# A Fourier-operator kernel on one Trainium2 core: the sum over h as two matmuls on 64-column tiles of the array instead of one on all 128 columns

## The chip, the core and the metric

One core of one Trainium2 chip runs the whole program. The metric is device microseconds of one execution. A core has a tensor engine (PE; its weight loads are listed apart, as PEld), a vector engine (DVE), a scalar engine (ACT), POOL, and SP, which here only starts DMAs. [...]

## What is computed

The input is x of shape (2, 56, 128, 128): 2 x 56 = 112 images of 128 x 128. Two layers, each x = x + conv(gn(x)), all in float32. Cut to what matters:

```python
def spectral_conv(x, w, b):            # 32 x 16 Fourier modes are kept
    xf = rfft2(x, norm='forward')
    of[:, :, :16, :16]  = einsum('bihw,iohw->bohw', xf[:, :, :16, :16],  w[0])
    of[:, :, -16:, :16] = einsum('bihw,iohw->bohw', xf[:, :, -16:, :16], w[1])
    return irfft2(of) + b
def fno_layer(x, ...):                 # spectral_conv + 1x1 skip, with norm and gelu as asked
def conv(x):
    xn = inorm(x)                      # per image
    k, q, v = fno_layer(xn) three times, 8 heads
    out = softmax(q k / 128) v         # attention over the 56 images of a batch entry
    out = fno_layer(out)
    att = inorm(out + x); an = inorm(att)
    h = gelu(inorm(spec(an)) + skip(an))      # M0
    h = inorm(spec(h)) + skip(h)              # M1
    return inorm(h) + att
```

## The kernel before

All planes stay in SBUF as `[h, image, w]`: X is the residual, A the work plane, 112 images each. Everything linear is carried in the 32 x 16 modes, so a plane is transformed forwards three times in a layer (for attention, M0 and M1) and back three times. A transform is two sums, each a matmul with a constant matrix of cosines and sines.

`to_rows` (line 265) is the first sum, over h. For eight images at a time it takes a PSUM tile `py` of 128 x 512 from the pool `pm` of four banks; for each image one matmul has the plane `A[:, i + e, :]` (128 x 128: h on partitions, w in columns) as the stationary operand and the constant `fh` (128 x 64: real and imaginary part of 32 rows of ky) as the moving one, and writes 64 columns of the tile with w on the 128 partitions (line 270). Then `evict` copies the tile to `Y`, on DVE (line 126) and ACT (line 128) in turn. `to_modes` (line 274) is the second sum, over w: eight matmuls of 32 output columns per half, on four column tiles of the array (line 282), then a swap of real and imaginary part (line 289). `from_modes` goes back: the modes are turned by way of DRAM (lines 300, 303), POOL copies a slice of 16 images (line 308), PE sums over ky with 64 x 64 stationary pieces on two column tiles (line 312), ACT evicts (line 316), PE sums over kx (line 319), and DVE uses the result.

In a layer, line 270 runs in four places. For each half of the images (a batch entry) come group norm (lines 340 to 364), row statistics (326), the instance norm that leaves A normalized (DVE line 378, two of three images, ACT line 376, the third), and `to_rows` of that half. I call the two halves A and B. In A, PE also has the group-norm sums of the second half (line 340) to do, which do not wait for `to_rows`; in B, the inner products of the first half (line 394: 128 weights of 56 columns, each streaming 56 columns, read with a stride of 512 bytes). After them come the scores (406), softmax, transposes (421, 446), the product with the attention (453), the mix of the images (462, 467), `from_modes`, statistics (253, 261), and the scales q1 and al (485 to 494). Then the places C (`to_rows` of all 112 images for M0) and D (the same for M1). Between them DVE adds att's part to the residual (line 538, once for each image) before it may write A again (line 542); both need q1.

A scheduler sets the order of each engine's instructions when the program is built, by its own estimate of times; semaphores then only make them wait.

Of the kernel before, what the change touches and what calls it, by code (L numbers as in the profile page):

```python
"""Two pre-activation CoDA-FNO layers on x (2, 56, 128, 128), float32 throughout, on one core.

A spectral convolution is a diagonal operator on 32 x 16 Fourier modes, so everything linear is
carried in those modes and in the image axis, and the 128 x 128 plane is touched only where the
layer is not low rank:

  xh      the instance-normed plane (mean 0); q, k, v = (Spec + s) (g1 xh + b1) + bias
  scores  <q_k, k_l> by Parseval = sum over modes of conj(xh_k) U xh_l  +  sq sk <xh_k, xh_l>
          with U = conj(wq + sq) (wk + sk) - sq sk
  out     the attention mixes images and Spec acts on modes, so they commute:  # L10
          P(attn v) = ISpec(sum_a T_a attn_a xh) + (sum_a sp sv attn_a) xh + constants
          with T = (wp + sp) (wv + sv) - sp sv
  M0, M1  the norm of Spec(x) is taken on its coefficients (its mean is the DC coefficient plus
          the bias M0b / M1b, which the norm subtracts again)

irfft2 takes the real part at kx = 0, which makes the multiplier there Hermitian:
w~(ky) = (w(ky) + conj w(-ky)) / 2, and w / 2 at ky = -16, whose mirror +16 carries the other half.
All of these are identities.

Layouts.  planes: [h, image, w].  modes: partition p = 32 j + 16 c + kx, free (t, image), where  # L20
c = re / im and 8 j + t is the row of ky in (0..15, -16..-1).
"""

# [15 lines left out]
I = B * K  # L39
HEADS = 8  # L40
EPS = 1e-5
HALF = 4 * I  # the images of four t: one PSUM bank

# [1 line left out]
_KY = np.r_[0:16, -16:0]  # L45
# [33 lines left out]

# columns of the vector of small parameters of a layer  # L80
_COLS = {}
# [9 lines left out]
N_W = 4 * HEADS + 2  # L91


def _bc(ap, axis, n):
    """A new axis of n repeats."""
    ap = ap.unsqueeze(axis)
    shape = list(ap.shape)
    shape[axis] = n
    return ap.to_broadcast(shape)
# [3 lines left out]
def fno_layers(ctx: ExitStack, tc: tile.TileContext, x, out, weights, small, const):  # L103
# [18 lines left out]
    def evict(to, of):  # L122
        """PSUM to SBUF, on the two engines in turn."""
        turn[0] ^= 1
        if turn[0]:
            nc.vector.tensor_copy(to, of)  # L126
        else:
            nc.scalar.copy(to, of)  # L128

# [1 line left out]
    X = planes.tile([N, I, N], F32, name="X")  # L131
# [29 lines left out]

# [1 line left out]
    def prepare(layer):  # L163
# [19 lines left out]

        # images' constants: c = b1 (w(0) + s) + bias
        c24 = col(24)
# [13 lines left out]
        g.tensor_tensor(pr["p_c"], pr["p_c"], par["psb"], ALU.add)  # L199
        # products of the skips' weights  # L200
        ss, vp = col(8), col(8)
# [9 lines left out]
        g.tensor_scalar(g2n, g2, float(N), None, ALU.mult)  # L211
        # w + s
        g.tensor_tensor(W[:, 0, 0:32, :], W[:, 0, 0:32, :], _bc(sm[:, 0:32], 2, 8), ALU.add)
# [32 lines left out]

# [1 line left out]
    def image_stats(rows, mu, var):  # L248
# [14 lines left out]

# [1 line left out]
    def to_rows(Y, i0, n):  # L265
        """The sum over h, of n images from i0: [w, (c, ky), image]."""
        for i in range(i0, i0 + n, 8):
            py = pm.tile([N, 512], F32, name="mm")
            for e in range(8):
                nc.tensor.matmul(py[:, 64 * e : 64 * e + 64], lhsT=A[:, i + e, :], rhs=fh, start=True, stop=True)  # L270
            evict(Y[:, :, i : i + 8].rearrange("p m i -> p i m"), py.rearrange("p (i m) -> p i m", m=64))

    def to_modes(Y):
        """The sum over w, and a copy with re and im exchanged."""
        xf = sp.tile([N, 8, I], F32, name="spec")
        xs = sp.tile([N, 8, I], F32, name="spec")
        pf = px.tile([N, 2, 512], F32, name="two")
        for h in range(2):
            for j in range(4):
                for c in range(2):  # L280
                    m = 32 * c + 8 * j + 4 * h
                    nc.tensor.matmul(
                        pf[32 * j : 32 * j + 32, h, :HALF], lhsT=fw[:, c, :], rhs=Y[:, m : m + 4, :],
                        start=(c == 0), stop=(c == 1),
                    )
            evict(xf[:, 4 * h : 4 * h + 4, :].rearrange("p t i -> p (t i)"), pf[:, h, :HALF])
        for h in range(2):
            ps = pm.tile([N, 512], F32, name="mm")
            nc.tensor.matmul(ps[:, :HALF], lhsT=swap, rhs=xf[:, 4 * h : 4 * h + 4, :], start=True, stop=True)
            evict(xs[:, 4 * h : 4 * h + 4, :].rearrange("p t i -> p (t i)"), ps[:, :HALF])  # L290
        return xf, xs

# [1 line left out]
    def from_modes(S, use):  # L294
        # ky from the free side to partitions and kx back, by way of memory
        turned = dram.tile([64, 16, I], F32, name="turned")
# [33 lines left out]

# [1 line left out]
    def layer(par, pr, last):  # L332
        mu, var, sd, rs, sh = (vec(n) for n in ("mu", "var", "sd", "rs", "sh"))
        Y = big.tile([N, 64, I], F32, name="big")
        for b in range(B):
            lo, hi = b * K, b * K + K
            # group norm over (image, h, 4 of w)
            acc = pa.tile([N, 512], F32, name="acc")
# [23 lines left out]
            for n, i in enumerate(range(lo, hi, 4)):  # L362
                e = nc.gpsimd if n % 3 == 2 else nc.vector
                e.tensor_tensor(A[:, i : i + 4, :], A[:, i : i + 4, :], gvf, ALU.mult)  # L364
                for k in range(4):
                    rows_stats(rows, i + k, i + k - lo)
            # instance norm: A = xh, with xa = sd xh + mu
            m_, v_, s_, r_, h_ = (t[:, lo:hi] for t in (mu, var, sd, rs, sh))
# [12 lines left out]

        # U xh for each head, while the tensor engine does <xh, xh>
        UX = big.tile([N, HEADS, 8, I], F32, name="big")
# [14 lines left out]

        # attention, rows k on partitions; then its transpose, rows l on partitions
        aT, pw = [], px.tile([N, 2, 512], F32, name="two")  # L400
        for b in range(B):
# [22 lines left out]
            aT.append(sT)  # L424
            # sum_a sp sv attn_a, transposed, as a block of the mix of all images
            wm = at.tile([K, HEADS, K], F32, name="scores")
# [9 lines left out]

        # D = sum_a T_a attn_a xh
        D = sp.tile([N, 8, I], F32, name="spec")
# [18 lines left out]

        # A = mix of the images, in place, four w at a time
        for w in range(0, N, 4):
# [9 lines left out]

        # A = out + xa  # L470
        rows2 = [st.tile([N, K, 6], F32, name="rows") for _ in range(B)]
# [7 lines left out]

        # att = q1 (A - mu) + ban;  an = alpha (A - mu) + b2  # L480
        mu, var, q1, al = (vec(n) for n in ("mu", "var", "q1", "al"))
# [12 lines left out]
        nc.vector.tensor_scalar(s0, al, par["m0sw"], None, ALU.mult)  # L494
        # t0 = m0sw b2 + m0sb - s0 mu;  ca = ban - q1 mu
        nc.vector.tensor_tensor(t0, s0, mu, ALU.mult)
# [7 lines left out]
        def normed(xf, xs, n, scale, dc):  # L504
            """The coefficients of inorm(Spec(scale x)), with dc in the place of the mean."""
            y = sp.tile([N, 8, I], F32, name="spec")
# [23 lines left out]

        # M0: A = gelu(inorm(Spec(an)) + m0sw an + m0sb)
        Y = big.tile([N, 64, I], F32, name="big")
# [3 lines left out]
        for i in range(I):  # L536
            # the residual takes att's part of A before A goes
            nc.vector.scalar_tensor_tensor(X[:, i, :], A[:, i, :], q1[:, i : i + 1], X[:, i, :], ALU.mult, ALU.add)
# [9 lines left out]

        # M1: A = inorm(Spec(h)) + m1sw h + m1sb
        Y = big.tile([N, 64, I], F32, name="big")  # L550
# [11 lines left out]

        # x + att + inorm(h, gmo, bmo)
        mu, var, a3, c3 = (vec(n) for n in ("mu", "var", "q1", "c3"))
# [27 lines left out]
def _weights(inputs, layer):  # L592
    """[p = (j, c, kx), own / mirrored in ky at kx = 0, re / im, weight, t]."""
    cols = []
    for n in ("K", "Q", "V", "P", "M0", "M1"):
        w = np.asarray(inputs[f"L{layer}_conv_{n}w"])
        w = w.reshape(2, -1, 16, 16, 2)
        cols.append(np.concatenate([w[0], w[1]], 1))  # weight, ky, kx, re / im
    w = np.concatenate(cols, 0)
    m = w.copy()  # L600
    m[:, :, 0] = w[:, (-np.arange(32)) % 32, 0]
    both = np.stack([w, m], 0).reshape(2, N_W, 4, 8, 16, 2)  # own, weight, j, t, kx, re / im
    one = both.transpose(2, 4, 0, 5, 1, 3)  # j, kx, own, re / im, weight, t
    two = np.stack([one, one], 1)  # j, c, kx, ...
    return two.reshape(N, 2, 2, N_W, 8)
# [34 lines left out]
```

## Time and profile before

| | |
|---|---|
| median of three runs | 1427.12 us |
| lowest and highest | 1420.92 and 1431.49 us |
| the profiled execution, span from its first to its last instruction | 1412.7 us |
| its mean granted TensorE clock | 0.747 |
| instructions | 13545 |
| line 270: multiplies, loads | 1344, 1344 |

The profile does not give the profiled execution a time of its own beside the span; 14.4 us lie between the span and the median of the runs. The clock is granted in two steps in this profile, 0.5 and 1.0 of full speed; the mean hides long stretches of either. In the profile's rows an instruction is named by line, engine, operation and `out<-in`, then partitions x elements. A pair such as `128*64` behind the tiles' names is rows x columns of the array that a load or multiply uses. The time behind a matmul's start goes to its modelled end and overlaps the next one's, so a pace is read from the starts of a run of them, or from the run's length without the last one's duration. Brackets hold the idle time before a row and what ended it.

### The profile page before, as it was taken

To read this page: it belongs to the slowest core of one execution; us is meant where nothing else is said; L and a number is where in the kernel's file an instruction comes from. 1 tells how busy PE (TensorE), PEld (TensorE's weight loads), DVE (VectorE), ACT (ScalarE), POOL (GpSimd) and SP (SyncE) were. 2 spreads that over 40 slices of the span, in tenths; PEclk is the share of its full clock that TensorE was granted. 3 is DMA by queue.
4 is the path that set the end of the run, shared out by engine and by line. 5 is a ranking of instruction groups with operands and counts; after the bars stand their busy time and mean duration, and the time that the engine had idled before them with its cause. 6 is when DMAs were issued, how large, how long until landed. Compare 5 with 4: busy or idle time off the path is not lost.

```text
span 1412.7 us, 13545 instructions
## 1 busy us (share of the span) xinstructions
PE 1003.7 (71%) x4992; PEld 695.5 (49%) x4992; DVE 819.8 (58%) x2052; ACT 306.0 (22%) x536; POOL 211.9 (15%) x259
## 2 busy tenths in 40 slices
PE   5374899798778936948633849989877887287550
PEld 1151788346664823724212438944566556146320
DVE  2367452791116797528978581739411397873498
ACT  0222200002221203410352321010122112152024
POOL 6603040000001013011131110400000001301102
PEclk9777599665558977979866957986555599599685
DMA  9000000001000010010000000000100000100106
GB/s 260 0 1 1 0 1 1 1 0 26 0 1 1 1 27 0 1 27 1 1 0 1 0 0 1 1 0 0 26 0 1 0 1 0 27 1 1 26 16 193
DMA packets 38872, 22.89 MB, mean 16 GB/s; under 512 B 8606, under 2 KB 37654, under 8 KB 38806
## 3 DMA queue, kind: packets, MB, share of 16 engines
q1 hardware_dynamic: 37216, 20.19, 5.8%
q10 hardware_dynamic: 1590, 1.83, 0.5%
q8 instruction: 39, 0.64, 0.2%
q14 instruction: 27, 0.22, 0.1%
HBM read 11.93 MB, written 10.09 MB: 16 GB/s over the span
## 4 chain that ended last, share of the span: by engine, by line
PE 60%; DVE 22%; ACT 8%; issue 3%; DMA 3%; POOL 3%; SPq 1%; ACTq 0%; POOLq 0%; DVEq 0%
PE mm L270 12%; PE acc L394 9%; PE mm L467 9%; PE mm L319 9%; DVE rows L326 6%; PE mm L453 5%; PE acc L353 3%; PE mm L312 3%; ACT t L464 3%; DVE A L364 2%; DVE A L580 2%; DVE A L557 2%; PE mm L462 2%; PE acc L340 2%; ACT A L128 2%
## 5 line engine op out<-in xcount | busy, mean ns | idle before, releaser
L319 PE MATMUL mm<-c_gw,t 128*128 128x512 f32 x336 | 168.8, 646 | 31.1 <-ACT t L316 31.1
L270 PEld LDWEIGHTS mm<-c_fh,A 128*128 128x128 f32 x1344 | 168.7, 206 | 8.5 <-issue 3.9
L270 PE MATMUL mm<-c_fh,A 128*128 128x64 f32 x1344 | 172.8, 291 | 0.0
L467 PE MATMUL mm<-mixT,t 112*128 112x112 f32 x512 | 131.2, 438 | 46.5 <-ACT t L464 46.5
L467 PEld LDWEIGHTS mm<-mixT,t 112*128 112x128 f32 x512 | 114.1, 328 | 72.8 <-ACT t L464 72.8
L308 POOL COPY lc<-spec 64x128 f32<-64x128 f32 x84 | 52.7, 655 | 627.7 <-PE mm L312 339.0
L126 DVE COPY A<-mm 128x448 f32<-128x448 f32 x32 | 29.1, 908 | 188.2 <-PE mm L467 188.2
L326 DVE BATCH_NORM_STATS2 rows<-A 128x6 f32<-128x128 f32 x672 | 137.0, 275 | 0.1
L394 PE MATMUL acc<-A 128*56 128x56 f32 x1024 | 134.0, 312 | 0.0
L394 PEld LDWEIGHTS acc<-A 128*56 128x56 f32 x1024 | 128.6, 226 | 6.1 <-issue 3.2
L319 PEld LDWEIGHTS mm<-c_gw,t 128*128 128x128 f32 x336 | 65.2, 205 | 108.1 <-issue 52.9
L126 DVE COPY big<-mm 128x512 f32<-128x512 f32 (+1 forms) x50 | 48.2, 971 | 98.6 <-PE mm L270 98.2
L312 PE MATMUL mm<-c_gh,lc 64*64 64x128 f32 x672 | 51.1, 297 | 75.0 <-POOL lc L308 75.0
L128 ACT COPY big<-mm 128x512 f32<-128x512 f32 (+1 forms) x50 | 47.8, 956 | 204.5 <-PE mm L270 138.9
L312 PEld LDWEIGHTS mm<-c_gh,lc 64*64 64x64 f32 x672 | 40.0, 145 | 104.0 <-POOL lc L308 76.1
L353 PE MATMUL acc<-t,ones_gn 128*128 128x512 f32 x112 | 57.1, 665 | 47.6 <-ACT t L352 47.6
L453 PE MATMUL mm<-attnT,big 56*128 56x448 f32 x128 | 82.8, 822 | 3.7 <-DVE spec L454 3.6
L542 DVE SCALAR_TENSOR_TENSOR A<-A,s,mm 128x128 f32<-128x128 f32 x224 | 59.4, 341 | 28.3 <-PE mm L319 28.3
L316 ACT COPY t<-mm 128x512 f32<-128x512 f32 x42 | 24.6, 586 | 220.6 <-PE mm L312 220.6
L462 PE MATMUL mm<-c_ident,A 128*112 128x128 f32 x256 | 68.0, 421 | 0.0
L340 PE MATMUL acc<-X,ones_gn 128*128 128x512 f32 x112 | 60.4, 688 | 10.1 <-DMA X<-x 7.6
L464 ACT COPY t<-mm 112x512 f32<-112x512 f32 x64 | 37.5, 586 | 136.5 <-PE mm L462 136.5
(170 smaller groups left out, 1239.9 us busy)
## 6 DMA issues: line engine op xcount, KB each, us to landing
X<-x SPq DMA_DIRECT2D x14, 512.0 KB, 7.3
out<-X SPq DMA_DIRECT2D x28, 256.0 KB, 2.3
turned<-spec SPq DMA_DIRECT2D x48, 56.0 KB, 2.0
spec<-turned SPq DMA_DIRECT2D x12, 224.0 KB, 3.7
raw<-weights ACTq DMA_DIRECT2D x2, 544.0 KB, 5.0
c_gw<-const_gw ACTq DMA_DIRECT2D x1, 256.0 KB, 5.3
sm<-small ACTq DMA_DIRECT2D x2, 63.0 KB, 5.5
c_swap<-const_swap ACTq DMA_DIRECT2D x1, 64.0 KB, 5.7
```

The costliest lines, as they stand in the source:

```text
L126: nc.vector.tensor_copy(to, of)
L270: nc.tensor.matmul(py[:, 64 * e : 64 * e + 64], lhsT=A[:, i + e, :], rhs=fh, start=True, stop=True)
L312: nc.tensor.matmul(pz[64 * c : 64 * c + 64, N * e : N * e + N], lhsT=four, rhs=gh[:, c, :], start=True, stop=True,)
L319: nc.tensor.matmul(po, lhsT=z[:, N * e : N * e + N], rhs=gw, start=True, stop=True)
L326: nc.vector.bn_stats(rows[:, k, :], A[:, i, :])
L340: nc.tensor.matmul(acc, lhsT=ones_gn, rhs=X[:, i : i + 4, :], start=(i == lo), stop=(i + 4 == hi))
L353: nc.tensor.matmul(acc2, lhsT=ones_gn, rhs=sq, start=(i == lo), stop=(i + 4 == hi))
L394: nc.tensor.matmul(acc[:K, :K], lhsT=plane, rhs=plane, start=(w == 0), stop=(w == N - 1))
L453: nc.tensor.matmul(pv, lhsT=XT[:, b, n, t, :], rhs=aT[b], start=True, stop=True)
L462: nc.tensor.transpose(pt[:I, N * e : N * e + N], A[:, :, w + e], ident)
L464: nc.scalar.copy(xt[:I, :], pt[:I, :])
L467: nc.tensor.matmul(po[:, I * e : I * e + I], lhsT=xt[:I, N * e : N * e + N], rhs=mix, start=True, stop=True)
```

## The change

In `to_rows` each image's matmul becomes two. The plane's 128 columns of w are halved; columns 0 to 63 go to the first 64-column tile of the array and to PSUM partitions 0 to 63, columns 64 to 127 to the second tile and to partitions 64 to 127. Both stream the same 64 columns of `fh`. What is computed, the PSUM tiles and the evictions are the same. All comments are gone from the file, too, which changes no instruction.

```diff
     def to_rows(Y, i0, n):
         for i in range(i0, i0 + n, 8):
             py = pm.tile([N, 512], F32, name="mm")
             for e in range(8):
-                nc.tensor.matmul(py[:, 64 * e : 64 * e + 64], lhsT=A[:, i + e, :], rhs=fh, start=True, stop=True)
+                for v in (0, 64):
+                    nc.tensor.matmul(
+                        py[v : v + 64, 64 * e : 64 * e + 64], lhsT=A[:, i + e, v : v + 64], rhs=fh, start=True, stop=True,
+                    )
             evict(Y[:, :, i : i + 8].rearrange("p m i -> p i m"), py.rearrange("p (i m) -> p i m", m=64))
```

Line 270 becomes line 271, and every line behind it is three higher in the changed file (340 is 343, 394 is 397, 538 is 541). The scheduler orders anew around the shorter pieces. A matmul in the lists below is one call; in the profile each such fp32 call is two loads and two multiplies. So `x16` on line 270 is sixteen images, and `x50` on line 271 is twenty-five.

PE in A, from the end of the first half's statistics. Before:

```order
L261 MATMUL acc<-dev,ones_var 128x112
L340 MATMUL acc<-X,ones_gn 128x512 x2
L270 MATMUL mm<-c_fh,A 128x64 x16
L340 MATMUL acc<-X,ones_gn 128x512
L270 MATMUL mm<-c_fh,A 128x64 x16
L340 MATMUL acc<-X,ones_gn 128x512 x3
L270 MATMUL mm<-c_fh,A 128x64 x24
L340 MATMUL acc<-X,ones_gn 128x512 x8
```

Now:

```order
L261 MATMUL acc<-dev,ones_var 128x112
L343 MATMUL acc<-X,ones_gn 128x512 x2
L271 MATMUL mm<-c_fh,A 64x64 x50
L343 MATMUL acc<-X,ones_gn 128x512
L271 MATMUL mm<-c_fh,A 64x64 x14
L343 MATMUL acc<-X,ones_gn 128x512 x2
L271 MATMUL mm<-c_fh,A 64x64 x48
L343 MATMUL acc<-X,ones_gn 128x512 x9
```

The group-norm sums of the other half still lie between the images, one more of them behind the last image. In B the same holds for line 394: 16 calls of it stand first, now followed by fourteen images without a break where there were eight, and the last 24 images stand together as before.

PE in C, behind the last of line 319. Before:

```order
L270 MATMUL mm<-c_fh,A 128x64 x57
L261 MATMUL acc<-dev,ones_var 128x112
L253 MATMUL acc<-rows,ones_mean 128x112
L270 MATMUL mm<-c_fh,A 128x64 x18
L261 MATMUL acc<-dev,ones_var 128x112
L270 MATMUL mm<-c_fh,A 128x64 x37
```

Now:

```order
L271 MATMUL mm<-c_fh,A 64x64 x99
L261 MATMUL acc<-dev,ones_var 128x112
L253 MATMUL acc<-rows,ones_mean 128x112
L271 MATMUL mm<-c_fh,A 64x64 x30
L261 MATMUL acc<-dev,ones_var 128x112
L271 MATMUL mm<-c_fh,A 64x64 x95
```

The statistics' small matmuls stand behind 49.5 and 64.5 images, where they stood behind 57 and 75.

DVE at the same place, up to the first row of line 538. Before:

```order
L126 COPY big<-mm 128x8x64
L262 TENSOR_REDUCE var<-acc 128x56
L254 TENSOR_REDUCE mu<-acc 128x56
L126 COPY big<-mm 128x8x64
L256 TENSOR_TENSOR dev<-rows,mu 128x112
L257 TENSOR_TENSOR dev<-dev 128x112
L258 SCALAR_TENSOR_TENSOR dev<-dev,rows 128x112
L126 COPY big<-mm 128x8x64
L262 TENSOR_REDUCE var<-acc 128x56
L126 COPY big<-mm 128x8x64
L485 RECIPROCAL q_2092<-q_2092 128x112
```

Now:

```order
L126 COPY big<-mm 128x8x64
L262 TENSOR_REDUCE var<-acc 128x56
L254 TENSOR_REDUCE mu<-acc 128x56
L256 TENSOR_TENSOR dev<-rows,mu 128x112
L257 TENSOR_TENSOR dev<-dev 128x112
L126 COPY big<-mm 128x8x64
L258 SCALAR_TENSOR_TENSOR dev<-dev,rows 128x112
L262 TENSOR_REDUCE var<-acc 128x56
L126 COPY big<-mm 128x8x64
L488 RECIPROCAL q_2204<-q_2204 128x112
```

The first row is the third eviction of C in both. The first row of line 538 stood behind all seven evictions and now stands behind the sixth. In A, B and D DVE's order is the same in both, and ACT's, POOL's and SP's are throughout.

## The prediction

> **What bounds the kernel now.** I read the page's shares, then the chain of waits, then the four places of a layer where line 270 runs.
>
> ```profile
> PE 1003.7 (71%) x4992; PEld 695.5 (49%) x4992; DVE 819.8 (58%) x2052; ACT 306.0 (22%) x536; POOL 211.9 (15%) x259
> PE mm L270 12%; PE acc L394 9%; PE mm L467 9%; PE mm L319 9%; DVE rows L326 6%; PE mm L453 5%; PE acc L353 3%; PE mm L312 3%; ACT t L464 3%; DVE A L364 2%; DVE A L580 2%; DVE A L557 2%; PE mm L462 2%; PE acc L340 2%; ACT A L128 2%
> ```
>
> Line 270 is the longest part of the chain that ended last. The four places in layer 0, each with the time of line 270's instructions alone, then the densest one (M1) on the timeline:
>
> ```profile
> core 0: us, PE busy (x) PEld busy (x), PEclk, DMA share, GB/s
> 80.40:107.80 27.40, 13.73 (x112) 14.02 (x112) 0.90 0.00 1
> 147.90:185.70 37.80, 22.38 (x112) 19.98 (x112) 0.60 0.00 0
> 471.00:497.00 26.00, 25.35 (x224) 25.18 (x223) 1.00 0.00 1
> 580.70:606.00 25.30, 25.12 (x224) 24.98 (x223) 1.00 0.01 1
> ...
> 580.76 25.12 PE L270 MATMUL mm<-c_fh,A 128*128 128x64 f32 x224
> 589.84 1.03 DVE L126 COPY big<-mm 128x512 f32<-128x512 f32 x1 [2.54 <-PE mm L270]
> 591.63 1.03 ACT L128 COPY big<-mm 128x512 f32<-128x512 f32 x1 [2.54 <-PE mm L270]
> ```
>
> I call them A and B (the halves of the images in attention), C (M0) and D (M1). Lines are those of the kernel before. One fp32 matmul is two loads and two multiplies in the trace (224 for 112 images). In D they follow each other every (25.12-0.28)/223 = 0.111 us, 0.223 us an image, and both evicting engines wait 2.54 us for PE each time. So D is PE alone.
>
> **What the 0.111 us is.** A multiply of 64 columns, or a load of 128? How long one multiply lasts to its end (ns, the middle number), by line:
>
> ```profile
> L270 PE MATMUL mm<-c_fh,A x1344: 219/275/476, 83.9 to 1291.7; 128*128 128x64 f32 x192
> L312 PE MATMUL mm<-c_gh,lc x672: 269/269/473, 428.8 to 1358.7; 64*64 64x128 f32 x168
> L406 PE MATMUL acc<-big,spec x64: 537/539/555, 240.2 to 938.4; 128*56 128x448 f32 x64
> L421 PE MATMUL mm<-c_ident,scores x32: 209/262/298, 252.3 to 947.5; 56*56 56x56 f32 x32
> L467 PE MATMUL mm<-mixT,t x512: 421/421/557, 314.1 to 1114.5; 112*128 112x112 f32 x171
> ```
>
> And the runs of them that price columns and loads:
>
> ```profile
> 240.20 12.21 PE L406 MATMUL acc<-big,spec 128*56 128x448 f32 x32
> 646.11 0.30 PEld L319 LDWEIGHTS mm<-c_gw,t 128*128 128x128 f32 x2 [0.98 <-ACT t L316]
> 646.64 0.19 PEld L319 LDWEIGHTS mm<-c_gw,t 128*128 128x128 f32 x1 [0.24 <-DVE A L557]
> 317.66 2.05 PE L467 MATMUL mm<-mixT,t 112*128 112x112 f32 x8 [0.67 <-ACT t L464]
> 314.00:430.00 116.00, 93.19 (x392) 80.25 (x394) 17.95 (x20) 32.68 (x48) 1.52 (x4) 0.50 0.04 8
> ```
>
> L406 streams 448 columns in (12.21-0.54)/31 = 0.376 us, 0.84 ns a column, so 64 columns need 0.054 us, half of the 0.111. Two loads of 128 columns that wait for nothing start 0.30-0.19 = 0.11 us apart: line 270 goes at the pace of its loads. Or load (0.056) and multiply (0.054) follow each other; the two readings cannot be told apart in line 270. L467 speaks for the first: at a granted clock of 0.50 eight take 2.05 us, (2.05-0.42)/7 = 0.23 us each, though 112 columns there stream in 0.19 us; a load after each would make 0.30 us.
>
> **The change part by part.** Per image it takes away two loads of 128 and two multiplies of 64 columns, and puts in four loads of 64 and four multiplies of 64 columns, half of them on either column tile. PE's instructions for the line double (2688 loads, 2688 multiplies); no eviction, DMA or other engine's instruction is added. In one tile a load of 64 is half of 0.11 us, 0.055, and its multiply 0.054. The nearest row with load and multiply of like size (56 and 56) is:
>
> ```profile
> 252.34 0.58 PE L421 MATMUL mm<-c_ident,scores 56*56 56x56 f32 x8
> ```
>
> (0.58-0.26)/7 = 0.046 to (0.58-0.21)/7 = 0.053 us each with the shortest and middle duration of this line, 0.052 to 0.060 for 64 columns. I take 0.056. The load is hidden behind the multiply there.
>
> Do two tiles run at once? The trace has both neighbours, two tiles of 64 columns (L312) and four of 32 (L282):
>
> ```profile
> 575.39 1.09 PE L312 MATMUL mm<-c_gh,lc 64*64 64x128 f32 x16
> 539.73 0.69 PE L312 MATMUL mm<-c_gh,lc 64*64 64x128 f32 x4 [24.69 <-POOL lc L308]
> 606.98 0.18 PEld L282 LDWEIGHTS two<-big,c_fw 128*32 128x32 f32 x8 [1.24 <-ACT big L128]
> 606.99 1.73 PE L282 MATMUL two<-big,c_fw 128*32 128x448 f32 x16 [1.10 <-ACT big L128]
> ```
>
> Sixteen multiplies of 128 columns one by one would be 16 x 0.108 = 1.7 us; L312 takes 1.09 us with the last one's 0.27: two at once. L282's sixteen of 448 columns would be 6.0 us and take 1.73: four at once, over all 128 rows. Eight loads of 32 columns would be 0.22 us in turn plus the end of one, and take 0.18: loads of different tiles overlap too. The bounds for a pair of tiles, two loads and two multiplies of 64 columns: 0.054 us (the stream alone), up to 0.109 us (L312's pair, if half the columns gained nothing). I take 0.056, since every row that is like in load and stream goes with the stream: **0.112 us an image for 0.223**, 0.111 saved (at half the clock 0.213 for 0.427).
>
> *D.* 112 x 0.111 = **12.4 us**. The evictions, 1.03 us for eight images on two engines in turn, now come every 0.90 us: 58% of each engine, still hidden.
>
> *C.* PE's chain from 471.15 to 496.86 is 25.7 us: 25.0 of line 270 and 0.6 of the norm's small matmuls. New: 12.5 + 0.6, and two waits that come up.
>
> ```profile
> 475.29 1.02 DVE L126 COPY big<-mm 128x512 f32<-128x512 f32 x1
> 477.37 0.28 DVE L258 SCALAR_TENSOR_TENSOR dev<-dev,rows 128x112 f32<-128x112 f32 x1
> 496.71 0.25 DVE L538 SCALAR_TENSOR_TENSOR X<-A,q,X 128x128 f32<-128x128 f32 x1
> 518.73 11.36 DVE L538 SCALAR_TENSOR_TENSOR X<-A,q,X 128x128 f32<-128x128 f32 x43
> ```
>
> DVE comes to its first eviction at 475.29, behind the statistics; with four PSUM buffers the fifth group waits for it until 476.3, when PE would be there at 471.15 + 4 x 0.90 = 474.75: 1.6 us. The second L261 then waits for DVE's second L258: in the new order four evictions and seven small operations stand up to its end, 475.29 + 4 x 1.03 + 7 x 0.28 = 481.4, and PE is there at 471.15 + 64.5 x 0.112 + 1.6 + 0.4 = 480.4: 1.0 us. So 25.7 - 15.7 = **10.0 us**. Late next is DVE: from 496.71 it works off 112 of L538 nearly without a gap, and L542 stands behind them. It cannot begin before q1, which waits for the same L261; in the new order the first one stands behind DVE's sixth eviction, and by the same kind of sum (two more evictions, two reciprocals and root of about 0.8 each, five small operations) starts near 486, 10 us sooner. The stretch moves as a whole.
>
> *A.*
>
> ```profile
> 82.14 9.83 DVE L378 TENSOR_SCALAR A<-A,rs,sh 128x128 f32<-128x128 f32 x38
> 100.64 7.08 PE L340 MATMUL acc<-X,ones_gn 128*128 128x512 f32 x16
> ```
>
> DVE's evictions stand behind its 38 normalizations, which end at 91.97. The fifth group's buffer is free 1.03 us later; then three groups (2.7) and eighteen multiplies of L340 at 0.43 (7.7): 103.4 for 107.7, **4.3 us** and not the 6 of the matmuls.
>
> *B.*
>
> ```profile
> 152.07 3.68 PE L270 MATMUL mm<-c_fh,A 128*128 128x64 f32 x16
> 155.68 0.48 PE L394 MATMUL acc<-A 128*56 128x56 f32 x2
> 156.09 1.54 PE L270 MATMUL mm<-c_fh,A 128*128 128x64 f32 x6
> 178.35 5.57 PE L270 MATMUL mm<-c_fh,A 128*128 128x64 f32 x48
> 198.72 23.48 PE L394 MATMUL acc<-A 128*56 128x56 f32 x188
> ```
>
> Here the clock is 0.5 until 178: 32 images cost 0.427 us each, the other 24 0.223. Saved: 32 x 0.213 + 24 x 0.111 = 9.5 us. L394 works in a 64-column tile as well, and the change from one form to the other shows: two of L394 take 0.41 us from 155.68 to the next L270 and 2 x 0.124 (23.48 us for 188) of work, 0.16 over; thirteen such turns, 2.1 us, which fall away when both have that form. PE is busy until L406 at 240, so it counts: **11.6 us**. DVE and POOL end the operands of L406 at 220.9, so 20 us of cover move along.
>
> A layer: 4.3 + 11.6 + 10.0 + 12.4 = 38.3 us. The second has the same rows. 1412.7 - 76.6 = 1336.1 us of span; the median of the runs lies 1427.1 - 1412.7 = 14.4 us above it, which I leave: **1350 us**.
>
> **The rivals.**
>
> *Load and multiply in series* (the second reading): 64 columns load in 0.028, a pair costs 0.084, an image 0.168. Saved per layer: 3.5 + 6.9 + 6.2 + 6.2 = 22.8 us, 1382 us. Against it stand L467 and L421.
>
> *No gain: the two tiles take turns at what bounds them.* If their loads do, 4 x 0.056 = 0.223 again and only the turns with L394 stay, 1423 us. L282's loads in 0.18 us speak against it. [...] Handing out the instructions can be such a turn as well:
>
> ```profile
> 77.68 0.50 PEld L253 LDWEIGHTS acc<-rows,ones_mean 128*128 128x128 f32 x2 [21.77 <-issue]
> 77.71 0.74 PE L253 MATMUL acc<-rows,ones_mean 128*128 128x112 f32 x2 [20.98 <-DVE rows L326]
> ```
>
> After a pause the multiply comes 0.03 us behind its load. At 0.031 each, eight instructions are 0.248 an image: 25 ns lost at full clock, 0.18 us won where the clock is half, about 1423 us as well. [...] L421's pair in 0.05 us speaks against it, though sixteen instructions may have stood ready.
>
> *Slower: a 64-column tile over 128 rows has its own price.* The only long stream of that form is L394, 0.124 us for 56 and 56 columns, at both clocks. If that came with the form and not with L394's stride of 512 bytes, and the tiles took turns, an image would be 4 x 0.124 = 0.496: 61 (C, D) + 14 (A) + 7 (B) = 82 us a layer, 1590 us. It decides above 0.253 us an image, where the half-clock stretch no longer pays for the rest. L394's stride is the more likely cause.
>
> **How the numbers follow.** A measurement of this kernel tells about 1% (14 us) from no change. The forecast 0.70, series 0.11, no gain 0.09, slower 0.10. The forecast's own range: 1335 (no new waits in A and C, 2 x 4.5 us, and the clock up before B's first group, 2 x 3 us) to 1366 (a pair at 0.068 us, 672 x 0.024 = 16 us more). The range must take in the series case and leaves out the other two: 1335 to 1405. Faster 0.81, same 0.09, slower 0.10.
>
> **What would show it.** In D 448 multiplies in about 12.8 us, the evicting engines' waits for PE near 0.8 us for 2.54; C some 16 us long with PE waiting for DVE near its start; in A a wait of PE for L126 before the last 24 images; in B no 0.16 us at the turns. If D shows 0.168 or 0.223 us an image with the loads evenly spaced, the price of the pair was wrong; if D is 12.8 us and the sum is not 77, a wait elsewhere took the rest.

## The result, and the profile after

The changed kernel takes **1327.5 us** (median of four runs, 1324.7 to 1330.0) where the kernel before took 1426.3 beside it (1420.9 to 1431.5): a ratio of **0.932, 95% interval 0.928 to 0.935**, 98.8 us less. The forecast was 1350, and its range reached down to 1335 only. The changed kernel's profiled execution took 1327.6 us, and its span is 1325.8 us, 86.9 less than the 1412.7 of before.

Busy time by engine and the chain of waits, from the page of the changed kernel:

```profile
PE 916.5 (69%) x6336; PEld 608.8 (46%) x6336; DVE 822.6 (62%) x2052; ACT 305.5 (23%) x536; POOL 207.8 (16%) x259
PE mm L470 10%; PE acc L397 10%; PE mm L322 9%; DVE rows L329 6%; PE mm L271 5%; PE mm L456 4%; PE acc L356 3%; PE mm L315 3%; ACT t L467 3%; DVE A L367 2%; DVE A L583 2%; DVE A L560 2%; PE mm L465 2%; PE acc L343 2%; ACT A L128 2%
```

The line was 12% of the chain, and is 5% of a shorter one. No other row has taken its place. The four places A, B, C, D of layer 0 again, each with the instructions of L271 alone (length of the stretch, busy time and count of multiplies, then of loads, granted clock):

```profile
82.00:103.70 21.70, 7.61 (x224) 7.00 (x224) 0.94 0.01 2
143.80:164.00 20.20, 9.64 (x224) 9.23 (x224) 0.86 0.01 2
450.80:467.00 16.20, 14.26 (x448) 13.57 (x448) 1.00 0.02 4
549.50:563.00 13.50, 13.24 (x448) 13.11 (x448) 1.00 0.01 4
```

Twice as many instructions take about half the time in all four. In B the clock is 0.86 where it was 0.60. D on the timeline, with two of the evictions (copies of a PSUM tile by DVE or ACT):

```profile
549.46 13.29 PE L271 MATMUL mm<-c_fh,A 128*64 128x64 f32 x448
558.13 1.03 DVE L126 COPY big<-mm 128x512 f32<-128x512 f32 x1 [0.83 <-PE mm L271]
559.06 1.04 ACT L128 COPY big<-mm 128x512 f32<-128x512 f32 x1 [0.83 <-PE mm L271]
```

So a load and multiply come every (13.29 - 0.22)/447 = 0.029 us, an image costs **0.117 us**, and the evicting engines' waits are down from 2.54 to 0.83 us. In the records the multiplies start alternately 6 and 52 ns apart, two together every 58 ns. One tile's pair thus takes 0.058 us (forecast 0.056), and two tiles run at once.

Where the span went, each place from the operation that starts it to the one that ends it, read off both traces in the same way (A: from the first half's variance, L262, to the reduction behind the second half's group norm, L344; B: from the second half's L262 to the first multiply of the scores, L406; C and D: from the first multiply of line 270 to the first of L312 behind it):

| place | before, layer 0 / 1 | after, layer 0 / 1 | saved | forecast |
|---|---|---|---|---|
| A | 27.1 / 26.7 us | 21.4 / 21.4 us | 5.7 / 5.3 us | 4.3 us |
| B | 92.2 / 92.2 | 76.5 / 76.6 | 15.7 / 15.6 | 11.6 |
| C and behind it | 68.7 / 68.7 | 57.8 / 57.8 | 10.9 / 10.9 | 10.0 |
| D and behind it | 55.8 / 55.5 | 43.8 / 43.7 | 12.0 / 11.8 | 12.4 |

The four places save 87.9 us, and the span is 86.9 us shorter; all other places together are 1.0 us longer. The remaining 98.8 - 86.9 = 11.9 us do not show in these two spans at all. In C, PE's own stretch fell from 25.9 to 16.0 us, by 9.9; the rest of C's 10.9 comes behind it.

**A** does not wait as the forecast had it. Its last groups, each of which starts with a weight load:

```profile
90.65 1.89 ACT L128 COPY big<-mm 128x512 f32<-128x512 f32 x2
92.41 1.95 PEld L271 LDWEIGHTS mm<-c_fh,A 128*64 128x64 f32 x64 [0.76 <-issue]
93.46 3.62 DVE L126 COPY big<-mm 128x512 f32<-128x512 f32 x4
94.54 1.01 PEld L271 LDWEIGHTS mm<-c_fh,A 128*64 128x64 f32 x32 [0.18 <-DVE big L126]
95.62 7.99 PE L343 MATMUL acc<-X,ones_gn 128*128 128x512 f32 x18
```

The fifth and sixth group start at 92.41, a microsecond before DVE's first eviction begins at 93.46. They write the two buffers that ACT has emptied by then. Only the seventh waits for DVE, 0.18 us.

**C** has short waits where the forecast had 1.6 and 1.0 us. PE's rows, and DVE's first row of L541, the addition to the residual (L538 before):

```profile
450.84 3.02 PE L271 MATMUL mm<-c_fh,A 128*64 128x64 f32 x96
454.06 2.08 PE L271 MATMUL mm<-c_fh,A 128*64 128x64 f32 x64 [0.21 <-ACT big L128]
456.35 1.38 PE L271 MATMUL mm<-c_fh,A 128*64 128x64 f32 x38 [0.20 <-ACT big L128]
460.64 0.47 PE L261 MATMUL acc<-dev,ones_var 128*128 128x112 f32 x2 [0.31 <-DVE dev L258]
461.05 5.81 PE L271 MATMUL mm<-c_fh,A 128*64 128x64 f32 x190
465.81 0.86 DVE L541 SCALAR_TENSOR_TENSOR X<-A,q,X 128x128 f32<-128x128 f32 x3
```

Here too buffers come from ACT (0.21 and 0.20 us), and the second L261 waits 0.31 us for DVE. L541 begins 465.81 - 450.84 = 15.0 us after C's start, where L538 began 496.71 - 470.99 = 25.7 us after it: 10.7 us sooner. Its 112 additions end 56.8 us after C's start for 67.8, and L315 (L312 before) starts 1.0 us behind them in both profiles: what stands behind C follows DVE.

**B** differs in two ways. The granted clock goes up at 149.6 us, 5.7 us after B's start, where it took 30 us before; and where L271 and L397 take turns they overlap. First two windows of all engines with the clock (the third number from the end), then one turn:

```profile
143.90:149.60 5.70, 5.70 (x67) 5.70 (x69) 5.22 (x21) 4.55 (x12) 0.00 (x0) 0.50 0.01 3
149.60:174.00 24.40, 24.19 (x336) 20.40 (x334) 11.49 (x29) 8.31 (x15) 1.64 (x1) 1.00 0.01 2
```

```profile
150.29 0.31 PE L397 MATMUL acc<-A 128*56 128x56 f32 x1
150.30 0.33 PE L271 MATMUL mm<-c_fh,A 128*64 128x64 f32 x2
150.41 0.30 PE L397 MATMUL acc<-A 128*56 128x56 f32 x1
150.53 0.53 PE L271 MATMUL mm<-c_fh,A 128*64 128x64 f32 x10
```

Two multiplies of L271 start within 0.01 us of one of L397, at 150.30 behind 150.29, and fit in before its next at 150.41. L397 writes rows 0 to 55 of its PSUM tile; that the two stand on the other column tile is the author's reading, since the rows do not name the tile. Counted from each multiply's start to the next one's, line 270's part of B fell from 21.5 to 8.7 us and L394's from 65.6 to 62.6.

### The profile page after: what moved, and what is told of

Its sections match the earlier page's. It is cut to its first block, busy times and chain, and to the rows that moved or that the text cites. A ratio compares the mean times of both kernels' runs of the same rounds, so it can differ in the third digit from the quotient of the medians.

```text
span 1325.8 us, 16233 instructions
## 1 busy us (share of the span) xinstructions
PE 916.5 (69%) x6336; PEld 608.8 (46%) x6336; DVE 822.6 (62%) x2052; ACT 305.5 (23%) x536; POOL 207.8 (16%) x259
## 4 chain that ended last, share of the span: by engine, by line
PE 54%; DVE 26%; ACT 9%; issue 4%; DMA 3%; POOL 2%; SPq 1%; ACTq 0%; POOLq 0%; DVEq 0%
PE mm L470 10%; PE acc L397 10%; PE mm L322 9%; DVE rows L329 6%; PE mm L271 5%; PE mm L456 4%; PE acc L356 3%; PE mm L315 3%; ACT t L467 3%; DVE A L367 2%; DVE A L583 2%; DVE A L560 2%; PE mm L465 2%; PE acc L343 2%; ACT A L128 2%
## 5 line engine op out<-in xcount | busy, mean ns | idle before, releaser
L311 POOL COPY lc<-spec 64x128 f32<-64x128 f32 x84 | 48.9, 608 | 631.2 <-PE mm L315 341.6
L397 PE MATMUL acc<-A 128*56 128x56 f32 x1024 | 130.5, 311 | 0.0
L397 PEld LDWEIGHTS acc<-A 128*56 128x56 f32 x1024 | 128.0, 227 | 3.2 <-issue 3.2
L315 PE MATMUL mm<-c_gh,lc 64*64 64x128 f32 x672 | 51.1, 297 | 71.2 <-POOL lc L311 71.2
L271 PEld LDWEIGHTS mm<-c_fh,A 128*64 128x64 f32 x2688 | 86.0, 140 | 11.6 <-DVE A L381 4.0
L271 PE MATMUL mm<-c_fh,A 128*64 128x64 f32 x2688 | 89.6, 226 | 1.3 <-ACT big L128 1.2
L315 PEld LDWEIGHTS mm<-c_gh,lc 64*64 64x64 f32 x672 | 40.0, 145 | 100.0 <-POOL lc L311 72.3
L343 PE MATMUL acc<-X,ones_gn 128*128 128x512 f32 x112 | 61.3, 697 | 11.2 <-DMA X<-x 9.0
L541 DVE SCALAR_TENSOR_TENSOR X<-A,q,X 128x128 f32<-128x128 f32 x224 | 67.3, 363 | 0.0
```

The costliest lines, as they stand in the source:

```text
L271: nc.tensor.matmul(py[v : v + 64, 64 * e : 64 * e + 64], lhsT=A[:, i + e, v : v + 64], rhs=fh, start=True, stop=True,)
L315: nc.tensor.matmul(pz[64 * c : 64 * c + 64, N * e : N * e + N], lhsT=four, rhs=gh[:, c, :], start=True, stop=True,)
L343: nc.tensor.matmul(acc, lhsT=ones_gn, rhs=X[:, i : i + 4, :], start=(i == lo), stop=(i + 4 == hi))
L397: nc.tensor.matmul(acc[:K, :K], lhsT=plane, rhs=plane, start=(w == 0), stop=(w == N - 1))
```

## The experiments

Ratios are to the kernel before on the same chip. The runs come from several chips, on which the kernel before had medians of 1420.4 to 1426.3 us, so times of different chips are compared by their ratios. Three questions stood: what lies in the 11.9 us, what raised the clock in B, and what exactly a pair of tiles runs at.

**1. The kernel before, once more.** No edit.

> The kernel before, unchanged, to see what lies between span and time. Forecast's reading: 14.4 us lie outside the span in every execution, so with a span of about 1412 the time is about 1427. Rival: only 1.7 us lie outside, as in the changed kernel (1327.6 for a span of 1325.8), and the spans themselves go from one execution to another by some 12 us; then a time of 1425 shows a span of 1423, and the place of the difference is to be seen in the granted clock of the stretches (0.5 up to 178 us in B of the first profile).

Measured: 1422.0 us median of ten (1411.7 to 1428.8), ratio 0.998 (0.995 to 1.002). In all ten the time is 1.7 to 1.8 us above the span, and the spans go from 1409.9 to 1427.0. The profiled one has a span of 1421.2 us, 8.5 over the first profile; 5.9 of that are layer 0's B, 98.1 us for 92.2, and 1.5 its C, 70.2 for 68.7. Its windows:

```profile
148.40:178.00 29.60, 29.60 (x160) 26.94 (x161) 12.63 (x43) 9.74 (x22) 0.00 (x0) 0.50 0.00 1
178.00:193.00 15.00, 15.00 (x81) 13.34 (x83) 1.01 (x1) 2.03 (x2) 0.00 (x0) 0.50 0.00 1
193.00:246.50 53.50, 53.50 (x426) 50.45 (x419) 28.52 (x19) 1.29 (x3) 19.20 (x8) 1.00 0.00 1
```

The clock came up 44.8 us after B's start, not 29.9. The same 48 multiplies that the forecast quotes with 5.57 us at 178.35 take here

```profile
178.68 10.50 PE L270 MATMUL mm<-c_fh,A 128*128 128x64 f32 x48
```

What follows: of the forecast's 14.4 us outside the span only 1.7 lie there. The profile that it worked from was one of the shortest executions, and the median's span is some 12 us longer. For 5.9 us of the difference between two executions the clock in B is shown to be the cause; for the longest ones (spans of 1427 us, 6 us more, as if both layers' B were late) there is no profile, and that is left open.

**2. The same work, one tile after the other.** Against the changed kernel:

```
-            for e in range(8):
-                for v in (0, 64):
+            for v in (0, 64):
+                for e in range(8):
```

> The same loads and multiplies, but the eight images of a group first all on the left column tile, then all on the right one. Theory (two tiles at once, each with its load hidden behind its own multiply): a tile alone takes 0.058 us for a load and multiply, so an image 0.233 us, D 26 us as before the change, and the time about that of before, 1425 to 1435. Rival 1 (a load hides only behind the multiply of the other tile): a tile alone takes 0.055 + 0.054, an image 0.42 us or, with a load of half the price, 0.33; D 37 to 48 us, 1490 or more. Rival 2 (shorter loads alone pay, the order does not matter, or TensorE reaches over the sixteen multiplies in between): D 13.2 us, 1327.

Measured: 1373.4 us (1371.3 to 1375.0), ratio 0.966 (0.960 to 0.971). D of layer 0:

```profile
564.02 21.51 PE L271 MATMUL mm<-c_fh,A 128*64 128x64 f32 x448
```

That is (21.51 - 0.22)/112 = 0.190 us an image, between 0.117 and the 0.233 of two tiles in turn. The starts of D's first multiplies tell why (ns from the first one):

```
0 106 165 223 281 340 398 456 515 573 631 690 748 754 806 861 865 919 923 977 1036 1094
```

A tile alone starts a multiply every 58 ns, load included: a load of 64 columns does hide behind the multiplies of its own tile, and 58 ns is the tile's own pace. Rival 1 falls. Near the change to the other tile, from 748 to 977, two multiplies start together three times: TensorE begins with the next tile some three multiplies early, and gains 3 x 58 ns at each change, not more. So Rival 2 is right for about a third of the step from 0.233 to 0.117 us, and the alternating order is what brings the rest. B took 79.3 and 79.9 us, little more than the changed kernel's 76.5, since its clock came up 4.4 and 5.7 us after its start too. For these two reasons the time stayed well below the theory's 1425 to 1435.

**3 and 4. The split in B alone, and in all but B.** Against the changed kernel, `step` is 64 (split) or 128:

```
-    def to_rows(Y, i0, n):
+    def to_rows(Y, i0, n, step):
...
-                for v in (0, 64):
+                for v in range(0, N, step):
```

with `64 if b else N` in attention and `N` in M0 and M1 for the third kernel, and `N if b else 64` and `64` for the fourth.

> The split in B alone; A, C and D keep the 128-column loads. Theory (the split form itself brings the clock up in B): the granted clock reaches 1.0 within 10 us of B's start, B takes 77 us for 92, the time is about 2 x 15.7 us under before, 1395. Rival (what went before B, a shorter A, brings the clock up): the clock stays 0.5 for some 30 us of B as in the kernel before, and B saves the forecast's 11.6 us, 2 x 11.6: 1403.

> The split in A, C and D, and the 128-column loads in B. Theory (the split form brings the clock up): B stays 92 us with the clock at 0.5 for some 30 us; saved are 2 x (5.9 + 10.9 + 11.8) = 57 us, 1369. Rival (a shorter A does): the clock in B is up after 6 us though the form is the old one, B takes some 86 us, and the time is about 1357.

Measured: 1387.0 us (ratio 0.975, 0.969 to 0.981) with B alone, 1362.9 (0.959, 0.953 to 0.965) without it. The clock at B's start in layer 0, of the third and then of the fourth kernel:

```profile
150.00:154.00 4.00, 4.00 (x36) 4.00 (x37) 3.52 (x14) 2.84 (x8) 0.00 (x0) 0.51 0.00 0
154.00:184.00 30.00, 29.79 (x406) 26.00 (x403) 17.66 (x37) 10.66 (x19) 6.34 (x3) 1.00 0.01 2
```

```profile
143.30:173.30 30.00, 30.00 (x163) 27.34 (x164) 12.65 (x43) 9.74 (x22) 0.00 (x0) 0.50 0.00 1
173.30:190.00 16.70, 16.70 (x90) 13.87 (x88) 1.64 (x2) 2.03 (x2) 0.00 (x0) 0.51 0.00 1
190.00:242.00 52.00, 52.00 (x414) 49.62 (x413) 27.92 (x18) 1.28 (x3) 19.26 (x8) 0.93 0.00 1
```

With the split in B alone the clock is up after 3.9 and 5.6 us, B takes 75.7 and 76.4 us, A, C and D what they took before. With the split everywhere else it is up after 46.5 and 30.1 us, and B takes 98.6 and 92.2. So the form used in B raises the clock, and the shorter A does not. By the medians B is worth 1425.0 - 1387.0 = 38.1 us, the rest 62.2; together 100.3 for the 98.8 of the whole. By the two profiles B was worth 15.7 + 15.6 = 31.3 us, from which the theory had its 1395 for run 3; the 6.8 us between fit a B that is longer in most executions than in the first profile, but run 3's interval is some 8 us wide to either side.

**6. More multiplying, with the old loads.** Is it the form of the load, the count of instructions, or the share of time in which the array multiplies? Against the kernel **before**, in B alone (`wide`), with `fh2` the transform twice side by side:

```
-                nc.tensor.matmul(py[:, 64 * e : 64 * e + 64], lhsT=A[:, i + e, :], rhs=fh, start=True, stop=True)
+                m = 128 if wide and e < 7 else 64
+                nc.tensor.matmul(py[:, 64 * e : 64 * e + m], lhsT=A[:, i + e, :], rhs=fh2[:, :m], start=True, stop=True)
```

> The kernel before, with 128-column loads everywhere; in B the multiply streams 128 columns (the transform twice) in place of 64 for seven of eight images, and the second half is overwritten by the next image. So B does more multiplying and no less loading, the opposite of a saving. Theory (the clock comes up when the array multiplies without pause, and loads that it waits for do not count): the array now streams 0.108 us for each load of 0.111, the clock is up within 10 us of B's start, and B is shorter than before: about 80 us for 92 to 98, the time 1400 or less. Rival (the form of the load, or the count of instructions, brings the clock up): it stays at 0.5 for 30 us or more, B takes 92 to 100 us, the time 1425.

Measured: **1393.7 us** (1392.8 to 1396.4), ratio 0.980 (0.978 to 0.982): a kernel that streams almost twice the columns in B is 2% faster than the one it was made from. Its windows and its first wide multiplies:

```profile
141.20:147.20 6.00, 6.00 (x41) 5.90 (x42) 5.55 (x22) 4.87 (x13) 0.00 (x0) 0.51 0.00 0
147.20:177.00 29.80, 29.80 (x243) 25.91 (x242) 16.02 (x29) 8.11 (x14) 6.63 (x4) 1.00 0.01 1
```

```profile
145.24 8.24 PE L274 MATMUL mm<-fh,A 128*128 128x128 f32 x64
```

The clock is up after 5.9 and 5.6 us, and B takes 82.7 and 82.5 us. Line 270's part of B is 13.7 us for 21.5 to 26.4 of before. (The compiler's order of B changed a little as well: L394's multiplies stand in longer runs, which is 1.7 us of the gain. C took 71.6 us for 68.7 to 70.2, which was not followed up.) The rival falls: the form and the number of loads are the old ones. Nor is it the longer runs: in run 1 48 multiplies of the old form in one piece, 10.5 us, left the clock at 0.5. What differs, by an estimate from L406's 0.84 ns a column and line 270's pace in B, is that the array now multiplies nearly all the time, where it did so half the time (64 x 2 x 0.84 = 108 ns of streaming for a multiply every 0.213 us at half the clock).

With the split tiles or the wide stream in B the clock came up 3.9 to 6.0 us after B's start (5.7 and 6.0 in the changed kernel, 4.4 and 5.7 in run 2, 3.9 and 5.6 in run 3, 5.9 and 5.6 in run 6); with the old form TensorE was 100% busy by the profile for 30 to 46 us at half the clock (29.9 in the first profile, 44.8 in run 1, 46.5 and 30.1 in run 4). So the profile's busy share does not tell the two apart, and the estimated share of streaming does.

Rows of the kernel before show that the share of multiplying time is not all there is to it:

```profile
265.47 24.26 PE L453 MATMUL mm<-attnT,big 56*128 56x448 f32 x32
266.60:287.10 20.50, 20.50 (x28) 9.11 (x28) 17.48 (x19) 0.00 (x0) 0.00 (x0) 0.50 0.00 1
172.52 5.90 PE L394 MATMUL acc<-A 128*56 128x56 f32 x46
174.50:177.90 3.40, 3.40 (x30) 3.40 (x30) 0.00 (x0) 0.00 (x0) 0.00 (x0) 0.50 0.00 0
177.90:181.30 3.40, 3.40 (x32) 3.31 (x30) 0.00 (x0) 0.92 (x1) 0.00 (x0) 1.00 0.00 0
```

The first two rows: L453 multiplies without pause, one every 0.75 us, as long as 448 columns take at half the clock (448 x 2 x 0.84 ns = 0.75 us, an estimate from L406's pace), and the clock stays at 0.50; it uses 56 rows of the array (`56*128`), where line 270 uses 128.

The other three: L394 uses 128 rows, streams about three quarters of its time at half the clock (56 x 2 x 0.84 = 94 of 124 ns, an estimate from the same pace), and at the end of its run of 46 the clock came up. In run 1 the same run, from 172.85, did not bring it up. In the clock records of the kernel before and of the changed one all changes lie whole multiples of 3.41 us apart; a whole step (174.5 to 177.9) fits into the run in the first profile, and none does in run 1 (steps from 172.6 and from 176.1, counted back from the change at 193.1). If a whole step is what counts, which is the author's guess, this would explain why B's clock is late by different amounts; no run tests it, nor the part of the rows; and in run 1 a run of 32 of L394 covers a whole step, from 148.7, without raising the clock, so L394 can at best lie at the edge. Nor does the old form bring the clock down: in C and D of the kernel before it runs at 1.00 for 25 us.

**5 and 8. Four tiles.** Against the changed kernel, four tiles of 32 columns; in the eighth kernel each multiply streams 128 columns as well:

```
-                for v in (0, 64):
+                for v in (0, 32, 64, 96):
...
-                        py[v : v + 64, 64 * e : 64 * e + 64], lhsT=A[:, i + e, v : v + 64], rhs=fh, start=True, stop=True,
+                        py[v : v + 32, 64 * e : 64 * e + 64], lhsT=A[:, i + e, v : v + 32], rhs=fh, start=True, stop=True,
```

> Four 32-column tiles an image in place of two of 64. Theory (a tile takes 0.058 us for 64 streamed columns whatever it loads, and as many tiles run at once as the program puts side by side): four at once, 8 x 0.058 / 4 = 0.117 us an image, D 13.1 us as with two, 1327. Rival 1 (0.029 us a multiply is the pace at which multiplies are handed out): 8 x 0.029 = 0.233, D 26 us, the time about that of the tile-by-tile run or worse, 1375 to 1425. Rival 2 (TensorE starts early only over some three multiplies that stand behind a busy tile): between the two, D 15 to 22 us.

> Four 32-column tiles an image, as in the run before with four, but each multiply streams 128 columns (the transform twice) in place of 64 for seven of eight images; the second half is overwritten by the next image. There every 128 multiplies took 1.8 us and were followed by a pause of 1.75 to 2 us in which TensorE waited for nothing that the profile shows, 3.73 us in all for 256 instructions, with one 16 KB packet on the instruction queue each time. Theory (instructions come at 256 in about 3.7 us at most): twice the streaming fills the pauses, a group of eight images still takes some 3.7 to 3.9 us, D some 54 us as with four tiles of 64 columns, the time 1360 to 1385. Rival (the pause of 1.8 us belongs to each group of images, whatever else it does): 3.4 + 1.8 = 5.2 us a group, D 20 us longer, C the same, the time 1440 or more.

Measured: 1367.5 us (ratio 0.961, 0.959 to 0.963) with 64 columns streamed, 1380.4 (0.973, 0.970 to 0.976) with 128. D of the fifth kernel, with the DMA packets of the instruction queue in 560.0 to 585.8, and D of the eighth:

```profile
566.88 1.99 PE L271 MATMUL mm<-c_fh,A 128*32 128x64 f32 x128 [1.58 <-issue]
570.61 1.99 PE L271 MATMUL mm<-c_fh,A 128*32 128x64 f32 x128 [1.73 <-issue]
...
578.34 1.99 PE L271 MATMUL mm<-c_fh,A 128*32 128x64 f32 x128 [1.74 <-issue]
```

```profile
q8 instruction: 7, 0.11, 2.0%
```

```profile
573.53 3.48 PE L275 MATMUL mm<-fh,A 128*32 128x128 f32 x128 [0.52 <-issue]
577.26 6.94 PE L275 MATMUL mm<-fh,A 128*32 128x128 f32 x255 [0.24 <-issue]
```

The theory of the fifth run held inside a stretch and failed over the whole: 128 multiplies (sixteen images, not a group of eight as the second expectation calls it) take 1.99 us, 0.014 us each, 0.112 us an image, four tiles at once. Then TensorE stops. The instruction queue shows one packet of 16 KB for each such stretch (0.11 MB in seven), and a stretch's 128 loads and 128 multiplies are 256 instructions. From the second stretch on, one follows the other after 3.57 to 4.00 us, 3.75 on average. Twice the streaming fills the pause instead of adding to it: the stretches of run 8 follow each other after 4.00, 3.73 and 3.46 us, with 0.5 us and less left idle, and D goes from 54.5 only to 55.8 us. So the pauses go with the count of instructions, **256 in about 3.7 us**, not with a group of images; the packet for each stretch points to their supply. On average that is Rival 1's 0.029 us a multiply, and run 5's 1367.5 us lie near its 1375 to 1425, but it comes in blocks and is not an even pace: inside a stretch a multiply takes 0.014 us. The changed kernel's D stands just at that rate, 64 pairs of multiplies x 58.3 ns = 3.73 us for 256; run 2 shows that its pace is the tiles' own.

**7. The products of planes on two tiles.** L397 was the largest line left to TensorE in B, 0.124 us a multiply. Against the changed kernel:

```
-                plane = A[:, b * K : b * K + K, w]
-                nc.tensor.matmul(acc[:K, :K], lhsT=plane, rhs=plane, start=(w == 0), stop=(w == N - 1))
+                plane, v = A[:, b * K : b * K + K, w], 64 * (w % 2)
+                nc.tensor.matmul(acc[v : v + K, :K], lhsT=plane, rhs=plane, start=(w < 2), stop=(w >= N - 2))
...
-            nc.scalar.copy(gram, acc[:K, :K])
+            odd = at.tile([K, K], F32, name="odd")
+            nc.scalar.copy(odd, acc[64 : 64 + K, :K])
+            nc.vector.tensor_tensor(gram, acc[:K, :K], odd, ALU.add)
```

> The changed kernel, and in it the products of the planes with themselves (56 and 56 columns, 512 bytes apart) put on the two column tiles in turn, even w left, odd w right, the two sums added at the end. Theory (the 0.124 us of such a load and multiply is the price of one tile, and tiles run at once): 0.062 each, B's 512 of them 32 us for 63, and B ends when the vector engine's products of modes do, some 21 us sooner: 1327 - 42 = 1285. Rival (columns 512 bytes apart share one way into the array, for both tiles): 0.124 as before, the time 1327 to 1330.

Measured: **1304.3 us** (1303.8 to 1307.0), ratio 0.917 (0.915 to 0.919). B takes 62.5 us in both layers.

```profile
173.99 22.07 PE L397 MATMUL acc<-A 128*56 128x56 f32 x310
207.24 9.14 PE L411 MATMUL acc<-big,spec 128*56 128x448 f32 x16 [11.18 <-DVE gram L401]
```

A multiply comes every 22.07/310 = 0.071 us for 0.124. The price of the strided form is a tile's price for the most part: two tiles that cost each other nothing would give 0.062. But 11.2 us of the gain turn into a wait for DVE, whose products of modes now end at 207 instead of 199.5. B is 14 us shorter in either layer, and the profiled span by 22.0 us, as 6 come back elsewhere, 4.4 of them between B and C; 42 were expected.

**9. And GpSimd's half of those products on DVE.** Against the seventh kernel:

```
-            nc.gpsimd.tensor_tensor(t, xs, _bc(pr["U"][1][:, a, :], 2, I), ALU.mult)
+            nc.vector.tensor_tensor(t, xs, _bc(pr["U"][1][:, a, :], 2, I), ALU.mult)
```

> The kernel with the products of the planes on two tiles, and in it the second products of modes (eight of 128x896 a layer) on the vector engine in place of GpSimd. There TensorE waited 11 us in B for the vector engine, whose operations of this size took 1.08 us before GpSimd began and 2.1 to 2.4 us beside it. Theory (the two slow each other down; alone the vector engine takes 1.08 us each): 24 x 1.08 = 26 us from 173, so the operands of the scores are there by 200 for 207; B 55 to 56 us for 62.5, the time 1304 - 14 = 1290. Rival (2.1 us is what such an operation takes once it reads what others have written): 24 x 2.1 = 50 us, B 78 us, 1335.

Measured: **1296.7 us** (1293.5 to 1300.3), ratio 0.914 (0.911 to 0.917); B 58.5 and 58.3 us.

```profile
182.25 1.34 DVE L389 TENSOR_TENSOR big<-spec,U_re 128x896 f32<-128x896 f32 x1
191.80 1.32 DVE L389 TENSOR_TENSOR big<-spec,U_re 128x896 f32<-128x896 f32 x1
195.49 1.09 DVE L389 TENSOR_TENSOR big<-spec,U_re 128x896 f32<-128x896 f32 x1
198.50 1.08 DVE L389 TENSOR_TENSOR big<-spec,U_re 128x896 f32<-128x896 f32 x1
...
202.86 12.60 PE L411 MATMUL acc<-big,spec 128*56 128x448 f32 x29 [7.10 <-DVE gram L401]
```

One engine alone is faster than the two beside each other, as the theory had it, by 4 us a layer and not 7: an operation takes 1.3 to 1.5 us until 195.5, after one of 2.4 at 174.4, and 1.08 from 195.5 on, and L397 ends at 195.8. This is the fastest version tried: 0.914 for the changed kernel's 0.932, some 25 us less by the ratios.

## Why the prediction was too high

The mechanism of the split was right: two tiles run at once, and each hides its loads. Steps around it were not. The sum was 1336.1 + 14.4 = 1350.5 before it was rounded, 23.0 us over the result; the parts are:

- **"The median of the runs lies 1427.1 - 1412.7 = 14.4 us above it, which I leave": 12.7 us.** Time and span differ by 1.7 to 1.8 us in every execution (run 1). The rest is that the profiled execution was a short one. A saving worked out in it was carried over to the longer ones as if the difference lay outside the kernel, but much of it lies in B at half the clock, just where the change acts (5.9 of the 8.5 us between two profiles in run 1); the changed kernel's four executions spread less, by 5.3 us for the 10.6 of the four beside them.
- **"Here the clock is 0.5 until 178: 32 images cost 0.427 us each", B: 4.1 us a layer, 8.1 in all.** The forecast priced the new multiplies at half the clock as well (0.213 us an image), as if the clock's course were given; a clock that comes up at once stood only as an end of the range, 2 x 3 us. In B it went with the work: with the split form the clock was up 3.9 and 5.6 us after B's start (run 3), with the old loads and a wide stream after 5.9 and 5.6 (run 6), with the old form after 46.5 and 30.1 (run 4). Line 270's part of B fell by 12.8 us instead of 9.5. The 2.1 us for turns with L394 were 3.0: the two now overlap (150.29 and 150.30 in the rows of B).
- **"The fifth group's buffer is free 1.03 us later", A: 1.2 us a layer, 2.4 in all.** Buffers were counted round in turn, while groups five and six in A take the two that ACT had emptied: only the seventh group waits for DVE, and only that one is left to do behind it.
- **"So 25.7 - 15.7 = 10.0 us", C: 0.9 us a layer, 1.8 in all.** PE's stretch fell by 9.9 us, as forecast, but by parts that made up for each other: waits of 0.7 us where 2.6 were put down (0.2 twice for ACT, 0.3 for DVE), against pairs and small matmuls that took longer. What follows goes by DVE's first row of L538, and for that the forecast's own sum (486 for 496.71) had 10.7 us, as measured; it took the 10.0 for both.
- **"I take 0.056", the pair.** It measured 0.058 us (D 13.3 us for 12.8). D won 11.9 us instead of 12.4, 1.0 us in all the other way, and other places gave back 1.0.

The first of these put the result outside the range. For waits that do not come the range had left 9 us, for an early clock 6; but the 14.4 us stood in it without a width. With 1.7 in their place the same sum gives 1350.5 - 12.7 = 1337.8, inside.

The rivals: *series* (0.168 us an image) is refuted by the tile alone in run 2, 58 ns with its load. *No gain* did not happen with two tiles, but its second mechanism, the handing out of instructions, has a counterpart: with four tiles 256 of them took 3.5 to 4.0 us whatever they streamed (runs 5 and 8), 0.014 to 0.016 us each, not 0.031, and in blocks. The *slower* case rested on L394's 0.124 us; a 64-column tile has no such price over dense columns (0.058 us in run 2), and even the strided ones go twice at once at 0.071 us (run 7).

Of what was to be seen, D's pace, the evicting engines' 0.83 us and C's 16 us came as written, and B's turns of 0.16 us are gone; the waits named for A and C did not come as named: A's is 0.18 us before the last eight images, C's first two are for ACT.

## What to carry to other kernels

A matmul that waits for its weight load can be split into column tiles that alternate from one multiply to the next: here a tile alone took 0.058 us for 64 columns with its load (run 2), and two in turn brought an image from 0.223 to 0.117 us. Count instructions before splitting further, since here 256 of them took about 3.7 us, and four tiles gave back most of what two had won in D (54.5 us for 43.8 with two and 55.8 before). Before pricing anything by the granted clock, ask whether the change alters it, and compare the profiled execution's own time with the spread of the runs before calling their difference overhead.

## What the chip showed that was not expected

- In B the clock did not follow TensorE's being busy: the first stretch ran 30 to 46 us at half the clock with TensorE busy 100% by the profile, and 3.9 to 6.0 us with the forms that by the estimate stream nearly all the time, among them one with more work (run 6). Multiplying without pause over 56 rows of the array, 24 us of L453, ran at 0.50.
- TensorE started multiplies of the other column tile some three multiplies (3 x 58 ns) before a run on the first one ended (run 2), and no earlier.
- The vector engine was slower while two tiles read planes at 512-byte steps: its 128x896 products took mostly 1.3 to 1.5 us beside them in run 9 and 1.08 us from 195.5 on, and in the changed kernel one took 1.08 us beside the same products on one tile:

```profile
172.13 1.08 DVE L389 TENSOR_TENSOR big<-spec,U_re 128x896 f32<-128x896 f32 x1
```

No run takes this apart further.
